# The first samples of a four-layer pipeline get another timetable, and their statistics another place

## The chip, the core and the metric

The kernel runs on one core of a Trainium2 chip. The core's engines work side by side and each has its own list of instructions, which it takes strictly in order: TensorE (PE, matrix products; its weight loads are shown apart as PEld), VectorE (DVE), ScalarE (ACT), GpSimd (POOL), and SyncE (SP), which here only issues DMAs. ACT and POOL issue some DMAs too. The metric is device time in microseconds (us). Three executions of the kernel before took 5671.38, 5691.11 and 5691.64 us, so the median is 5691.11 us.

## The reference

The input x has 16 samples of 64 x 64 positions (4096 tokens) with 256 channels, in float32. Four layers follow one another, each as x = x + layer(group_norm(x)), with 32 groups of channels whose mean and variance run over a whole sample. That is why each layer needs statistics of the whole sample before it can begin.

```
x = x + codebook(gn(x))       # nearest of 1024 codes per token: argmin of the distance, then the code
x = x + rowattention(gn(x))   # f, g, h = x Wf + bf, x Wg + bg, x Wh + bh; sigmoid(f g^T) h along each image row
x = x + gate(gn(x))           # x0, x1, x2 = x w1, x w2, x w3; softmax over n of x0[n] x1[m];
                              # gate = sigmoid(sum_n x2[n] softmax[n, m]); gate * x
x = x + linattention(gn(x))   # q, k, v; softmax of q over a head's channels, of k over tokens;
                              # context = k v^T; context q; W_out; layer norm with gamma and beta
```

## The kernel before

A sample's tokens are worked on in 8 chunks of 512. Each sample goes through seven stages, and each stage is a Python generator that emits some instructions and yields a number of steps:

- **statistics** (`stats0`): loads the 8 chunks of the input, 512 KB each, on SP's queue into the pool `xb` (4 buffers), two `bn_stats` of VectorE per chunk (L266), then `gn_finish` (L270 to L299) on all engines, with small matrix products and a `pow` on GpSimd. Its result, `norm0[b]`, is needed by the search of that sample.
- **search** (`stage1`, L330 on): per tile of 128 tokens four products of 128 x 512 (L403), ScalarE's bias (L398), VectorE's maximum and its index (L409, L414), and an indirect DMA on POOL's queue that adds the chosen code to the token (L415). `back` (L371 on) transposes the sums (L378), takes their statistics and stores them. 32 tiles.
- **layer 1** (`layer1`, L436 on): the row attention, matrix products L482, L493, L513 and L533, and one VectorE addition per chunk (L538). It loads chunk `ch + 2` when chunk `ch` is done, into a pool of 3 buffers (`xm`).
- **rows** (`rows2`): the three rows x0, x1, x2. It loads the 8 chunks again, into the same pool `xb` as the statistics.
- **exps** (`stage2`): 64 times ScalarE's exponential of 128 x 2048 elements (L645) and VectorE's weighted sum (L648).
- **gate** (`gate2`): multiplies x by its gate (L702, L703).
- **layer 3** (`stage3`): the linear attention, most of its work in matrix products (L765, L782, L902, L908).

A planner at the end of the program gives each stage of each sample a start and a length on a clock of its own, whose unit is one search: search b runs from b to b + 1. A stage starts at its ready time or when the same stage of the sample before ends, whichever is later. A heap then always advances the generator that is due first, by its yield times length over total. So the planner decides the order of the program, not times. The order is a priority: the framework builds each engine's list from it by taking, in a model of the machine, the earliest instruction in program order that is ready. The constants: layer 1 begins 0.06 after its search and takes 0.7 (0.2 for sample 0), rows 0.1, the exponentials start 0.17 after layer 1's end and take 1.0, the gate 0.8, layer 3 1.0. `FILL` places the statistics of samples 1 to 7 (two from 0.05 to 0.95, three from 1.0 to 1.27, two from 1.4 to 1.58). Those of samples 8 to 15 start at b - 0.7 and take 0.5.

With these numbers the first exponentials are due from 1.43 to 2.43, those of sample 1 from 2.93 to 3.93 (they wait for layer 1 of that sample), and from then on the exponentials of one sample follow those of the other without a gap.

Of the kernel before, what the change touches and what calls it, by code (L numbers as in the profile page):

```python
# [22 lines left out]
NCHUNK = NT // CH  # L23
CW = CH * P
# [9 lines left out]
LAGR = 0.03  # L34
# [3 lines left out]
LEN3 = {0: 0.4, 1: 0.33, 2: 0.37}  # L38
FILL = ((0.05, 0.95, 2), (1.0, 1.27, 3), (1.4, 1.58, 2))
EARLY = sum(n for _, _, n in FILL)  # L40


@with_exitstack
def kernel(
# [265 lines left out]

    norm0 = {}

    def stats0(b):
        tag = f"s0_{b}"
        st = stats_tile(0, f"st_{tag}")
        src = xT[b].rearrange("(k p) n -> p k n", p=P)
        for ch in range(NCHUNK):
            xt = xb.tile([P, NK, CW], F32, tag="xb", name=f"xs_{tag}_{ch}")
            nc.sync.dma_start(out=xt, in_=src[:, :, ch * CW : (ch + 1) * CW])
            chunk_stats(st, xt, ch)  # L320
            yield 1.5
        with tc.high_priority(offset=URGENT):
            norm0[b] = gn_finish(st, "n0", b)
        yield 2


    x1_d, norm1 = {}, {}

    def stage1(b):
# [6 lines left out]
        def load(ch):  # L336
            xt[ch] = xa.tile([P, NK, CW], F32, tag="xa", name=f"xt_{tag}_{ch}")
            nc.sync.dma_start(out=xt[ch], in_=src[:, :, ch * CW : (ch + 1) * CW])

# [53 lines left out]
        for ch in range(NCHUNK):  # L393
            for t in range(CH):
# [24 lines left out]
                )  # L419
                yield 4  # L420
                if t == 1 and ch > 0:
                    back(ch - 1)
                    yield 2
# [17 lines left out]
    def layer1(b):  # L441
# [9 lines left out]
        def load(ch):  # L451
            xt[ch] = xm.tile([P, NK, CW], F32, tag="xm", name=f"xt_{tag}_{ch}")
            nc.sync.dma_start(out=xt[ch], in_=x1[ch])

# [95 lines left out]
        for ch in range(NCHUNK):  # L550
            if ch > 0:
                store(ch - 1)
            if ch + 1 < NCHUNK:
                yield from attend(ch + 1)
                yield 2
            mix(ch)
            yield 3
        store(NCHUNK - 1)
# [373 lines left out]
    tasks, free = [], {}  # L932
    b = 0
    for begin, end, n in FILL:
# [11 lines left out]
    for b in range(nb):  # L946
# [3 lines left out]
        task("search", b, 1.0, stage1(b), 160)  # L950
        end = task("layer1", b + 1 + LAG1, (LEN1 if b else 0.2) if left else 0.35, layer1(b), 88)
        task("rows", end + LAGR, 0.1, rows2(b), 8)
        if left:
            end = task("exps", end + LAG2, 1.0, stage2(b), 160)
            end = task("gate", end + LAG3, 0.15 if left == 1 else LENG, gate2(b), 36)
        else:
            end = task("exps", end + LAG2, 0.65, stage2(b, NCHUNK), 200)
# [47 lines left out]
```

## Time and profile before

| | |
|---|---|
| median of three executions | 5691.11 us (5671.38 to 5691.64) |
| the profiled execution | 5674.06 us, span 5672.1 us |
| TensorE / VectorE / ScalarE / GpSimd busy | 91% / 89% / 81% / 32% of the span |
| mean granted clock of TensorE | 0.962 |
| moved by DMA | 1059.26 MB, 187 GB/s over the span |
| exponentials of sample 0 begin, end | 322 us, 584 us |
| exponentials of sample 1 begin | 713 us |
| exponentials of sample 15 begin, end | 5224 us, 5507 us |

In the lines of the profile an instruction is named by its line in the kernel (L403), its engine, and its tiles as out<-in. A row of a table by stretches has the beginning and end of the stretch in us from the span's start, its length, the busy time of PE, PEld, DVE, ACT and POOL with the number of instructions in brackets, the granted clock of TensorE as a share of full speed, the mean busy share of the 16 DMA engines, and what they moved in GB/s. Where the table is of one tile alone, only the engines that touch it are listed. Durations of groups are merged busy time.

### The profile page before, as it was taken

How to read it: one execution, taken by the hardware profiler on the slowest of the kernel's cores; microseconds unless marked ns; L12 is line 12 of the kernel's file. 1: busy time of each engine (PE TensorE's matmuls, PEld its weight loads, DVE VectorE, ACT ScalarE, POOL GpSimd, SP SyncE). 2: the span in 40 equal slices, each digit the busy share in tenths (PEclk: the TensorE clock that was granted, in tenths of full speed). 3: DMA queues.
4: the chain of work that ended last, by engine and by line, in shares of the span. 5: the costliest groups of instructions: out<-in, count | busy, mean ns of one | idle time of the engine just before them, and what ended most of it. 6: DMA issues, size and time to landing. Idle time of an engine off the chain costs nothing.

```text
span 5672.1 us, 76096 instructions
## 1 busy us (share of the span) xinstructions
PE 5162.0 (91%) x26927; PEld 3189.6 (56%) x26927; DVE 5049.3 (89%) x7186; ACT 4571.1 (81%) x6642; POOL 1801.5 (32%) x1076
## 2 busy tenths in 40 slices
PE   7977889989999999999999999999999999987788
PEld 3534446545656566565655656565565656564556
DVE  7589799899999999999999999999999999988882
ACT  4468589888989898888978888898888879887873
POOL 2223234323333333334333333333333333321221
PEclk9988999999999999999999999999999999998889
DMA  8553744655665757566575656657575675745543
GB/s 254 174 178 84 232 115 144 214 163 185 196 198 175 224 159 236 171 211 198 185 234 155 216 185 200 210 173 236 160 224 183 201 219 156 222 149 176 200 157 119
DMA packets 521365, 1059.26 MB, mean 187 GB/s; under 512 B 52504, under 2 KB 266392, under 8 KB 512792
## 3 DMA queue, kind: packets, MB, share of 16 engines
q1 hardware_dynamic: 406288, 885.11, 46.5%
q0 software_dynamic: 73728, 67.14, 8.3%
q10 hardware_dynamic: 40968, 102.13, 4.6%
q8 instruction: 214, 3.51, 0.3%
q14 instruction: 167, 1.37, 0.1%
HBM read 751.18 MB, written 303.04 MB: 186 GB/s over the span
## 4 chain that ended last, share of the span: by engine, by line
PE 46%; DVE 17%; ACT 16%; issue 6%; DMA 5%; POOL 4%; SPq 0%; ACTq 0%; DVEq 0%; POOLq 0%
PE pd_s L403 14%; ACT ex_s L645 7%; DVE ex_s L648 7%; PE ph_l L493 4%; PE pxo_s L908 3%; PE pqv_s L782 3%; PE po_l L533 2%; PE pk_s L765 2%; ACT nn_s L398 2%; POOL qv_s L802 2%; PE pz_s L857 2%; DVE i_s L414 2%; DVE nn_s L409 2%; PE pxo_s L902 2%; PE pvr_s L865 2%
## 5 line engine op out<-in xcount | busy, mean ns | idle before, releaser
L648 DVE CUSTOM_DVE_ANT_0 ex_s<-ex_s,x2b 128x2048 f32<-128x2048 f32 x1024 | 2360.4, 2312 | 77.6 <-ACT ex_s L645 74.6
L645 ACT ACTIVATE ex_s<-x0b,nmax_s,x_r 128x2048 f32<-128x2048 f32 x1024 | 2138.6, 2089 | 40.7 <-DVE num_s L648 30.5
L403 PE MATMUL pd_s<-e,xn_s 128*128 128x512 f32 x4096 | 1971.1, 614 | 43.9 <-DVE m L409 27.9
L415 POOL DMA_INDIRECT xc_s<-in_emb_rows,i_s x512 | 1113.7, 2175 | 1852.7 <-DVE i_s L414 1337.5
L403 PEld LDWEIGHTS pd_s<-e,xn_s 128*128 128x128 f32 x4096 | 745.8, 195 | 778.8 <-issue 669.1
L409 DVE CUSTOM_DVE_ANT_0 nn_s<-pd_s,nn_s 128x1024 f32<-128x1024 f32 x512 | 619.9, 1212 | 113.5 <-PE pd_s L403 63.0
L414 DVE FIND_INDEX8 i_s<-m,nn_s 128x8 uint32<-128x1024 f32 x512 | 622.9, 1217 | 0.0
L398 ACT ACTIVATE nn_s<-ne,nx_s 128x1024 f32<-128x1024 f32 x512 | 582.5, 1143 | 33.1 <-DVE nx_s L369 18.7
L493 PE MATMUL ph_l<-wh_l,xt_l 128*128 128x256 f32 x2048 | 519.6, 390 | 28.7 <-DVE m L409 16.9
L782 PE MATMUL pqv_s<-wqv_s,xk_s 128*128 128x256 f32 x2048 | 489.3, 381 | 0.0
L493 PEld LDWEIGHTS ph_l<-wh_l,xt_l 128*128 128x128 f32 x2048 | 379.7, 192 | 138.9 <-issue 69.0
L782 PEld LDWEIGHTS pqv_s<-wqv_s,xk_s 128*128 128x128 f32 x2048 | 389.1, 191 | 120.6 <-issue 59.7
L802 POOL TENSOR_TENSOR qv_s<-qv_s,qm_s 128x512 f32<-128x512 f32 x128 | 221.6, 1731 | 662.6 <-DVE qm_s L801 363.2
L868 POOL TENSOR_TENSOR lrs_s<-lrs_s,mhalf 128x4 f32<-128x4 f32 x128 | 178.0, 1391 | 677.2 <-ACT lrs_s L867 663.3
L756 POOL TENSOR_TENSOR qv_s<-qv_s,qd_s 128x512 f32<-128x512 f32 x128 | 214.4, 1675 | 249.0 <-DVE qd_s L755 132.0
L533 PE MATMUL po_l<-blk,h_l 128*128 128x128 f32 x2048 | 282.1, 288 | 3.0 <-DVE m L409 1.5
L533 PEld LDWEIGHTS po_l<-blk,h_l 128*128 128x128 f32 x2048 | 260.6, 200 | 41.1 <-issue 24.5
L908 PE MATMUL pxo_s<-wctx_s,qo_s 128*128 128x256 f32 x1024 | 269.2, 386 | 2.2 <-DVE qo_s L876 2.2
L765 PE MATMUL pk_s<-xk_s,wk_s 128*128 128x512 f32 x512 | 256.0, 620 | 1.0 <-DMA xk_s<-x_g 0.9
L913 ACT COPY y_s<-pxo_s 128x512 f32<-128x512 f32 x256 | 147.5, 580 | 132.4 <-PE pxo_s L912 116.0
L378 PE MATMUL pt_s<-ident,xc_s 128*128 128x128 f32 x1024 | 156.7, 282 | 105.2 <-DMA xc_s<-in_emb_rows,i_s 79.0
L351 ACT ACTIVATE sq_s<-xt_s,first 128x512 f32<-128x512 f32 x256 | 200.2, 806 | 37.2 <-DMA x0b<-rows_r 21.0
(206 smaller groups left out, 7322.0 us busy)
## 6 DMA issues: line engine op xcount, KB each, us to landing
xs_s<-in_xT SPq DMA_DIRECT2D x128, 512.0 KB
xt_s<-in_xT SPq DMA_DIRECT2D x128, 512.0 KB
xc_s<-in_x SPq DMA_DIRECT2D x128, 512.0 KB
x_s<-xt_s ACTq DMA_DIRECT2D x128, 512.0 KB
xt_l<-x_s SPq DMA_DIRECT2D x128, 512.0 KB
x_l<-xt_l SPq DMA_DIRECT2D x128, 512.0 KB
xr_r<-x_l SPq DMA_DIRECT2D x128, 512.0 KB
xg_g<-x_l SPq DMA_DIRECT2D x128, 512.0 KB
```

What stands on the lines that cost most here:

```text
L398: nc.scalar.activation(nn, ne2, AF.Identity, bias=nx2[ch][:, t : t + 1])
L403: nc.tensor.matmul(pd[:, cols], lhsT=xn[ch][:, k, t * P : (t + 1) * P], rhs=e2[:, k, cols], start=(k == 0), stop=(k == NK - 1),)
L409: nc.vector.tensor_tensor_reduce(out=nn, in0=pd, in1=nn, scale=1.0, scalar=-3.0e38, op0=ALU.add, op1=ALU.max, accum_out=m8[:, 0:1],)
L414: nc.vector.max_index(i8, m8, nn)
L415: nc.gpsimd.indirect_dma_start(out=xc[ch][:, t, :], out_offset=None, in_=emb_rows, in_offset=bass.IndirectOffsetOnAxis(ap=i8[:, 0:1], axis=0),
L493: nc.tensor.matmul(ph[:, t, :], lhsT=X[:, k, t * P : (t + 1) * P], rhs=wh_n[:, k, :], start=(t % 2 == 0 and k == 0), stop=False, skip_grou ...
L533: nc.tensor.matmul(po[:, m : m + P], lhsT=h[:, t, k * P : (k + 1) * P], rhs=at[:, t, :, :].rearrange("p r i -> p (r i)"), start=True, stop ...
L645: nc.scalar.activation(ex, x0b, AF.Exp, bias=nmax[:, T : T + 1], scale=x01[:, T, 1:2], accum_out=den[:, h, T : T + 1])
L648: nc.vector.tensor_tensor_reduce(out=ex, in0=ex, in1=x2b, scale=1.0, scalar=0.0, op0=ALU.mult, op1=ALU.add, accum_out=num[:, h, T : T + 1],)
L765: nc.tensor.matmul(pk, lhsT=wk_n[:, k, :], rhs=xt[:, k, :], start=(k == 0), stop=(k == NK - 1))
L782: nc.tensor.matmul(pqv[:, j, :], lhsT=xt[:, k, t * P : (t + 1) * P], rhs=wqv_n[:, k, :], start=(j == 0 and k == 0), stop=False, skip_group ...
L908: nc.tensor.matmul(px[:, j, :], lhsT=qT[:, t * P : (t + 1) * P], rhs=wctx[:, 1, :], start=False, stop=False, skip_group_check=True,)
```

## The change

A table `RAMP` gives the first four samples their own numbers: the distance of layer 1 from its search, the length of layer 1, the length of rows, the distance of the exponentials from layer 1's end, and the length of the exponentials. On the planner's clock the exponentials of samples 0 to 3 now run from 1.31 to 2.56, 2.56 to 3.76, 3.76 to 4.90 and 4.90 to 5.98, each beginning where the one before ends. Layer 1 of samples 0 to 3 takes 0.15, 0.3, 0.45 and 0.58. From sample 4 on the numbers are the old ones, and exponentials, gate and layer 3 are due 0.05 later than before.

`FILL` is empty. The statistics are advanced from within sample 0's own stages: those of sample 1 from `stage1`, one step after certain tiles (9 steps within the first 28 tiles); those of samples 2 to 5 from `layer1`, 4 or 5 steps after each chunk (36 steps over 8 chunks). The loads of these statistics are tied on SP's queue behind the newest load of the search or of layer 1 (`issue_after`), so that they can't be issued ahead of it. The statistics of samples 6 and 7 now start at b - 0.7 like the later ones.

```diff
-FILL = ((0.05, 0.95, 2), (1.0, 1.27, 3), (1.4, 1.58, 2))
-EARLY = sum(n for _, _, n in FILL)
+RAMP = {0: (0.03, 0.15, 0.05, 0.13, 1.25), 1: (0.04, 0.3, 0.06, 0.14, 1.2), 2: (0.05, 0.45, 0.08, 0.16, 1.14), 3: (0.06, 0.58, 0.1, 0.17, 1.08)}
+FILL = ()
+BESIDE = (1, 4)
+EARLY = sum(BESIDE) + sum(n for _, _, n in FILL)
...
-    norm0 = {}
-
-    def stats0(b):
+    norm0, marks = {}, {}
+
+    def behind(name):
+
+        return tc.issue_after(marks[name]) if name in marks else nullcontext()
+
+    def stats0(b, after=None):
...
-            nc.sync.dma_start(out=xt, in_=src[:, :, ch * CW : (ch + 1) * CW])
+            with behind(after):
+                nc.sync.dma_start(out=xt, in_=src[:, :, ch * CW : (ch + 1) * CW])
...
+    beside = {
+        "search": chain.from_iterable(stats0(b, "search") for b in range(1, 1 + BESIDE[0]) if b < nb),
+        "layer1": chain.from_iterable(stats0(b, "layer1") for b in range(1 + BESIDE[0], 1 + sum(BESIDE)) if b < nb),
+    }
+
+    def advance(name, b, n):
+
+        for _ in range(n if b == 0 else 0):
+            next(beside[name], None)
...
-            nc.sync.dma_start(out=xt[ch], in_=src[:, :, ch * CW : (ch + 1) * CW])
+            marks["search"] = nc.sync.dma_start(out=xt[ch], in_=src[:, :, ch * CW : (ch + 1) * CW]).ins
...
                 yield 4
+                advance("search", b, ((T + 1) * 9 * BESIDE[0]) // 28 - (T * 9 * BESIDE[0]) // 28)
...
-            nc.sync.dma_start(out=xt[ch], in_=x1[ch])
+            marks["layer1"] = nc.sync.dma_start(out=xt[ch], in_=x1[ch]).ins
...
             mix(ch)
+            advance("layer1", b, ((ch + 1) * 9 * BESIDE[1]) // NCHUNK - (ch * 9 * BESIDE[1]) // NCHUNK)
             yield 3
...
-    b = 0
+    b = sum(BESIDE)
...
-        end = task("layer1", b + 1 + LAG1, (LEN1 if b else 0.2) if left else 0.35, layer1(b), 88)
-        task("rows", end + LAGR, 0.1, rows2(b), 8)
+        early, len1, lenr, early2, lenx = RAMP.get(b, (LAG1, LEN1, 0.1, LAG2, 1.0))
+        end = task("layer1", b + 1 + early, len1 if left else 0.35, layer1(b), 88)
+        task("rows", end + LAGR, lenr, rows2(b), 8)
...
-            end = task("exps", end + LAG2, 1.0, stage2(b), 160)
+            end = task("exps", end + early2, lenx, stage2(b), 160)
```

More of the change, by code (lines that the diff above doesn't have):

```diff
@@ L1 @@
 import heapq
-from contextlib import ExitStack
+from contextlib import ExitStack, nullcontext
+from itertools import chain
 import concourse.bass as bass
```

## The prediction

> **What bounds the kernel now.** I read first the page's head and its busy shares: TensorE (PE) is busy for 5162 us and VectorE (DVE) for 5049 us of a span of 5672.1 us, so neither leaves much to the other. Then I cut the span where one stage's work begins or ends. The marks are the first exponential of each sample (ScalarE's timeline: 322, 713, 1013, 1309, 1629, 1953, 2286 us, ... 5224 us for the last), the end of sample 0's exponentials (584 us) and the beginning of the second search (182 us).
>
> ```profile
> span 5672.1 us, 76096 instructions
> PE 5162.0 (91%) x26927; PEld 3189.6 (56%) x26927; DVE 5049.3 (89%) x7186; ACT 4571.1 (81%) x6642; POOL 1801.5 (32%) x1076
> ```
>
> The same stretches, busy time of each engine, granted clock, DMA share, GB/s:
>
> ```profile
> 38.00:182.00 144.00, 129.69 (x476) 60.48 (x475) 124.19 (x217) 69.85 (x93) 52.06 (x36) 0.99 0.83 240
> 182.00:322.00 140.00, 134.43 (x830) 81.11 (x830) 67.78 (x116) 60.33 (x118) 22.92 (x24) 0.96 0.55 178
> 322.00:585.00 263.00, 189.23 (x766) 94.68 (x765) 250.34 (x324) 214.85 (x259) 81.89 (x39) 0.87 0.40 117
> 585.00:713.00 128.00, 116.12 (x565) 61.25 (x564) 86.29 (x147) 64.50 (x102) 28.05 (x21) 0.97 0.79 252
> 713.00:1013.00 300.00, 277.96 (x1412) 162.66 (x1411) 274.02 (x380) 263.30 (x373) 105.17 (x56) 0.95 0.47 140
> 1013.00:1309.00 296.00, 266.43 (x1390) 156.95 (x1389) 280.29 (x372) 257.94 (x350) 89.57 (x48) 0.95 0.61 190
> 1309.00:1629.00 320.00, 309.03 (x1673) 192.66 (x1672) 304.42 (x432) 284.10 (x413) 113.44 (x64) 1.00 0.62 194
> 1629.00:1953.00 324.00, 311.71 (x1672) 193.69 (x1671) 304.04 (x428) 283.83 (x412) 113.93 (x64) 0.99 0.62 191
> 1953.00:2286.00 333.00, 317.30 (x1684) 197.52 (x1683) 315.07 (x446) 284.71 (x415) 112.83 (x66) 0.98 0.64 198
> 5224.00:5507.00 283.00, 217.09 (x995) 153.99 (x994) 240.14 (x351) 225.71 (x341) 71.27 (x46) 0.86 0.50 169
> ```
>
> The reader is to see an engine that changes. The first search is TensorE's. Layer 1 of sample 0 is TensorE's alone (134 of 140 us, VectorE half idle). The first exponentials are VectorE's (250 of 263 us, TensorE at 72% and its clock at 0.87). Then come 128 us without exponentials, in which VectorE idles for 42 us. From 1309 us on both are at 95%. VectorE's work on the tile of the statistics, by stretch:
>
> ```profile
> 38.00:182.00 144.00, 41.15 (x62) 0.99 0.83 240
> 182.00:200.00 18.00, 6.11 (x10) 0.81 0.57 168
> 322.00:585.00 263.00, 20.13 (x32) 0.87 0.40 117
> 1953.00:2286.00 333.00, 10.43 (x16) 0.98 0.64 198
> ```
>
> Sixteen instructions are one sample, about 10 us. Four of the seven early samples lie beside the first search, two in the stretch that VectorE bounds. A stretch with one sample of statistics takes 333 us, the one before it without took 324.
>
> **The work of a sample.** The groups' busy times, added by stage and scaled so that they meet the page's totals (TensorE's groups add up to 5836 us against 5162, factor 0.885; VectorE's 0.928, since groups overlap), over 16 samples. TensorE: search 2282 x 0.885 / 16 = 126 us; layer 1 with its norms and the rows pass 1400, 77 us; layer 3 2154, 119 us. VectorE: search 1510 x 0.928 / 16 = 88; layer 1 and norms 367, 21; exponentials 2485, 144; gate 367, 21; layer 3 565, 33; statistics 167, 10.
>
> **Check against before.** The planner's clock counts searches: search b runs from b to b+1. Before, the exponentials of sample 0 run from 1.43 to 2.43, those of sample 1 from 2.93 to 3.93, then one sample per unit without a gap. For each stretch I take the larger of the two engines' work. To 1: 126 (measured 144). To 1.43: 0.43 x 126 + 77 = 131 (140). To 2.43: VectorE 88 + 144 + 0.53 x 21 + 2 x 10 = 263 (263). To 2.93, the pause: 0.5 x 126 + 0.47 x 77 = 99 (128). To 3.93: VectorE 282 (300). To 4.93: 290 (296). Then 322 (320) and 322 (324). The sum is 1835 against 1915 measured between 38 and 1953 us. The 80 us on top are 18 in the first search, 9 in layer 1, 29 in the pause, 18 and 6 in the two stretches behind it.
>
> **The change, part by part,** up to the start of sample 5's exponentials. That is 6.98 on the new clock, 6.93 before; seven samples have their statistics by then in both.
>
> Statistics beside the first search: one sample instead of four. That takes 3 x 10 us of VectorE and 24 loads of 512 KB from a stretch whose DMA share is 0.83. TensorE waited 11.5 us there for gathered rows. The work left is TensorE's, so at most its 14 us of idle time go: between 0 and 14, I take 6, since the gather's wait is the part that traffic can lengthen. 138 us.
>
> Layer 1 of sample 0 (1.00 to 1.31 instead of 1.43): TensorE 0.31 x 126 + 77 = 116, plus the 9 seen before, 125. Four samples of statistics come in: 64 VectorE instructions, 40 us, under a VectorE that was busy for 68 of 140 us and loses 0.12 x 88 = 11. They are covered. Their 32 loads are less sure. The stretch moved 178 GB/s x 140 us = 24.9 MB; 0.12 of a search less is about 2 MB (1059 MB / 16 = 66 MB a sample, a quarter of it the search's); 32 loads of 512 KB less what of the old ones lay there add some 14. That is 37 MB; at 268 GB/s, the rate of the 50 us with the highest DMA share that held statistics loads, 138 us; at 313, the best slice, 118. I take 133, between the two bounds; ends 123 and 150.
>
> The Trainium skill, "DMA: Bandwidth & Descriptors", section Specifications, gives about 358 GB/s as a core's share of HBM. By that figure 37 MB would take an estimated 103 us, TensorE would decide, and this sum would be 8 us lower; no slice of this trace reaches it.
>
> Exponentials of sample 0 (1.31 to 2.56): VectorE 1.25 x 88 + 144 + 21 = 275, no statistics any more. TensorE 1.25 x 126 + 77 = 234. Layer 1 of sample 1 is now pressed into 2.04 to 2.34, and taken alone that part is TensorE's (0.34 x 126 + 70 = 113 against 89 on VectorE). In three parts the sum is 140 + 113 + 44 = 297. I take 290, near the upper end, since the pause showed that such alternation is not smoothed; ends 278 and 306.
>
> Exponentials of samples 1 to 4: 2.56 to 3.76, VectorE 1.2 x 88 + 21 + 144 + 21 + 10 = 302, plus 12 (18 and 6 before), 314. To 4.90: TensorE 1.14 x 126 + 77 + 0.94 x 119 = 333, plus 4, 337. To 5.98: TensorE 325, VectorE 322 with one statistics, plus 11 (333 measured for 322 and 317), 336. To 6.98: 314 plus 11, 325.
>
> A load of the statistics is issued on SP's queue behind the newest load of the search or of layer 1, and is itself held until VectorE frees one of four buffers; whatever SP issues next (the search's loads and tokens, layer 1's stores, the rows pass, which uses the same buffers) stands behind it. In the first search these issues waited 60.0 us for VectorE in 23 waits, 2.6 us each, and TensorE did not feel it. I price it at nothing: layer 1 loads two chunks ahead. If that cover is gone, it is the slower rival below.
>
> The Trainium skill, "SBUF — State Buffer", section "SBUF: two separate sides", says of DMAs issued from GpSimd that their descriptors starve while VectorE holds a port shared with it. In this trace TensorE waited 45.4 us for gathered rows between 330 and 585 us, where VectorE was at 95%, and 11.5 us in the first search; the rule speaks against longer exponentials beside the search. By it 45 x 1.25 = 56 us would be waited for by TensorE, which is what it has spare (290 - 234), so the sum would stay.
>
> **Sum.** 138 + 133 + 290 + 314 + 337 + 336 + 325 = 1873, against 1915: 42 us earlier, to a point where 0.05 of a search and layer 1 more is done. Behind it the clocks run alike (11.09 units to the end), with exponentials, gate and layer 3 0.05 later against the search. At the end no search covers that: 0.05 x 283 us, the last exponentials' stretch, is 14. Of that I take 12: from nothing, if VectorE's 43 us idle there absorb it, to 17 us, 0.05 of the last 697 us per 2.02 units. The profiled execution took 5674.06 us, 2 more than its span: 5674 - 30 = 5644. It lay 17 us under the median of three, 5691.11, and 3 over the fastest; I put the forecast between the two readings (5644 and 5661): 5652.
>
> **Rivals.** (1) No change within 0.5%: layer 1 at its DMA bound (150), the first exponentials at 306, and the planner's pause replaced by a new alternation, as the 297 warns: 30 - 17 - 16 is a loss of 3, 5677 to 5694, say 5682. For it speaks that VectorE's idle time before the first exponentials stays much the same: both the search's share and 20 us of statistics leave it. Against it, TensorE and VectorE are both better covered after 2.56. (2) Slower: SP's queue in layer 1 of sample 0. Between 26 and 199 us 40 loads of statistics were issued, 4.3 us apart. If the 32 new ones keep that pace and the 24 others of layer 1 and rows, 2 us each, add to it instead of filling in, the stretch takes 138 + 48 = 186 us and more, and every wait of VectorE for a chunk holds the search behind it; at 200 the gain of 30 is a loss of 37, 5674 + 37 = 5711 to 5728, say 5720. It decides from a stretch of about 190 us on. Against it: DVE waited for such a load for only 12.0 us in the whole run. (3) The change does not do what it says: instructions run ahead wherever an engine is free, so sample 0's exponentials end early as before and the pause comes back as idle VectorE time; then only the earlier start stays, 6 + 7 us, 5661 to 5678, say 5668.
>
> **How the numbers follow.** What a measurement of this kernel can tell is about 0.5%, 28 us. Chances: forecast 0.47, rival 1 0.20, rival 2 0.20, rival 3 0.13. Rival 3 and a shift of the steady stretches by 0.05, which no row prices (2 us per stretch over ten would be 20), fall on both sides of that line. So faster by over 0.5% 0.49, within it 0.28, slower 0.23. The range: with all lower ends (130, 123, 278, and 5 less in each of the other four) the sum is 50 us less, 5594 on the profiled execution and 5611 on the median, so 5600; upwards it takes in rival 1 and reaches to rival 2's 5720. The forecast's own range is 5610 to 5665.
>
> **What the profile after would show.** The statistics' tile: 16 instructions up to about 176 us, 64 in the next 133 us, none until about 1250. DMA share there near 0.9 instead of 0.55. First exponentials of the samples near 309, 599, 913, 1250, 1586 and 1911 us. No stretch of 100 us without an exponential before 5100. VectorE's idle time from 585 to 713 gone, and TensorE's clock above 0.87 during sample 0's exponentials. I am wrong if the first exponential comes after 340 us, if long waits of the DMA queue on the statistics appear in layer 1, or if the stretches after 1911 are longer than 335.

## The result, and the profile after

The changed kernel takes 5739.32 us (median of six executions, 5719.06 to 5744.57), the kernel before 5682.09 us (six executions, 5665.41 to 5691.64). The ratio is 1.0098, with a 95% interval from 1.0075 to 1.0122: slower by 1%. The prediction was 5652 us, its range 5600 to 5720.

The profiled execution of the changed kernel took 5719.06 us, the fastest of the six; the one of before took 5674.06. So the traces explain 45 of the 57 us between the medians, and everything that follows is told in those 45. The head of the page after:

```profile
span 5717.2 us, 76163 instructions
PE 5175.7 (91%) x26927; PEld 3211.8 (56%) x26927; DVE 5063.6 (89%) x7186; ACT 4575.3 (80%) x6642; POOL 1745.5 (31%) x1076
```

The work is the same: TensorE is busy for 13.7 us more, VectorE for 14.3 us, in a span that is 45 us longer. The time went into idle stretches of both. I cut the span at the first exponential of each sample, as for the kernel before. They now come at 333, 641, 956, 1301, 1651, 1986, 2328 us, ... 5026 and 5284 us; before, at 322, 713, 1013, 1309, 1629, 1953, 2286, ... 4958 and 5224. The table by stretches, columns as in the prediction:

```profile
38.00:181.00 143.00, 127.40 (x458) 59.27 (x457) 101.70 (x175) 68.96 (x90) 50.82 (x34) 0.97 0.57 154
181.00:333.00 152.00, 132.37 (x796) 80.95 (x794) 83.38 (x144) 54.26 (x110) 19.35 (x23) 0.92 0.67 224
333.00:590.00 257.00, 201.31 (x912) 105.62 (x913) 234.12 (x292) 222.26 (x270) 73.61 (x34) 0.89 0.38 107
590.00:641.00 51.00, 51.00 (x255) 26.37 (x254) 34.12 (x61) 22.87 (x42) 12.64 (x11) 1.00 0.70 232
641.00:956.00 315.00, 270.49 (x1286) 146.52 (x1285) 293.69 (x399) 269.69 (x361) 98.80 (x50) 0.92 0.55 169
956.00:1301.00 345.00, 329.97 (x1727) 203.09 (x1726) 318.85 (x451) 293.05 (x425) 121.56 (x70) 0.98 0.60 186
1301.00:1651.00 350.00, 328.16 (x1738) 203.72 (x1737) 323.51 (x465) 290.30 (x421) 121.68 (x69) 0.99 0.63 195
1651.00:1986.00 335.00, 312.87 (x1651) 193.03 (x1650) 314.26 (x447) 284.32 (x410) 107.44 (x65) 0.98 0.63 198
1986.00:2328.00 342.00, 319.28 (x1682) 199.83 (x1681) 312.45 (x445) 284.84 (x413) 102.56 (x67) 0.97 0.62 193
5284.00:5557.00 273.00, 211.17 (x958) 150.59 (x957) 245.57 (x347) 222.39 (x334) 68.06 (x44) 0.85 0.50 167
```

Three things are to be seen. The pause between the exponentials of samples 0 and 1 (590 to 641) shrank from 128 to 51 us. The exponentials of sample 0 (333 to 590) did not get longer: 257 us, before 263. And the four stretches behind them (641 to 1986) take 1345 us where they took 1240, with TensorE busy for 92% and VectorE for 93% of them, before 94% each. Before, TensorE had used the pause to work ahead (116 of 128 us busy) and the next stretches were short, 300 and 296 us. TensorE's work in the pause and the four stretches together is 1281 us before and 1292 after. The pause was time of TensorE's that the change moved rather than won.

The rows of the statistics' tile (VectorE alone) show that the placement was done as the diff says: 22 instructions in the first search, 56 beside layer 1, none beside sample 0's exponentials, and 16 each for samples 6 and 7 later.

```profile
38.00:181.00 143.00, 14.63 (x22) 0.97 0.57 154
181.00:333.00 152.00, 34.89 (x56) 0.92 0.67 224
333.00:590.00 257.00, 0.00 (x0) 0.89 0.38 107
...
1301.00:1651.00 350.00, 10.51 (x16) 0.99 0.63 195
1651.00:1986.00 335.00, 10.39 (x16) 0.98 0.63 198
```

The 45 us divide into three:

| part | before | after | difference |
|---|---|---|---|
| start to sample 5's first exponential | 1953 us | 1986 us | +33 |
| nine steady samples, 5 to 14 (one sample) | 3005 us (333.9) | 3040 us (337.8) | +35 |
| from sample 14's first exponential to the end | 714 us | 691 us | -23 |

In the nine steady samples both kernels do the same with the same instructions; only the planner's times of exponentials, gate and layer 3 are 0.05 of a search later. The whole stretch in one row, of the kernel before:

```profile
1953.00:4958.00 3005.00, 2836.25 (x15133) 1768.06 (x15132) 2815.36 (x3990) 2559.80 (x3723) 1029.14 (x592) 0.98 0.63 197
```

and of the changed kernel:

```profile
1986.00:5026.00 3040.00, 2844.12 (x15116) 1780.60 (x15115) 2821.16 (x3987) 2559.15 (x3717) 994.00 (x593) 0.97 0.62 194
```

TensorE is idle for 3005.00 - 2836.25 = 169 us before and for 196 us after: 27 of the 35 us are idle time, 8 are matrix products that took longer. What TensorE waited for in this stretch (who waited <- for what; us in total, times, the longest; pg_n at L285 before and L288 after is the group norm's first product), before:

```profile
PE px_s L357 <- ACT sq_s L351: 22.0, 26, 2.2
PE prt_r L602 <- ACT rows_r L597: 15.4, 8, 2.6
PE pxt_s L364 <- ACT xrow_s L362: 15.3, 25, 1.6
```

and after:

```profile
PE pg_n L288 <- DVE mv_n L284: 45.1, 9, 5.0
PE pd_s L421 <- DVE gate_s L676: 32.2, 8, 5.6
PE pc_s L827 <- ACT ek_s L815: 27.9, 28, 2.3
PE prt_r L622 <- ACT rows_r L617: 24.0, 9, 2.7
```

The two waits at the head of the list come once in nearly every sample, and neither was among the long ones before. The first is the group norm behind a search, which needs the statistics of that search's last chunk. One of its nine places in the timeline (start, duration; in brackets the idle time before it and the instruction that ended it):

```profile
2679.09 1.04 PE L396 MATMUL pt_s<-ident,xc_s 128*128 128x128 f32 x8
...
2680.86 1.06 ACT L399 COPY xt_s<-pt_s 128x512 f32<-128x512 f32 x2
2681.08 2.23 DVE L668 CUSTOM_DVE_ANT_0 ex_s<-ex_s,x2b 128x2048 f32<-128x2048 f32 x1
2683.23 1.28 DVE L269 BATCH_NORM_STATS2 st_s<-xt_s 128x6 f32<-128x512 f32 x2
2684.43 0.59 DVE L284 BATCH_NORM_AGGREGATE mv_n<-st_s 128x2 f32<-128x48 f32 x2
2685.16 0.56 PE L288 MATMUL pg_n<-mv_n,dmat 128*128 128x2 f32 x2 [5.04 <-DVE mv_n L284]
```

TensorE ends the last transposes at 2680.1 us and has the norm's product next in its list. ScalarE copies the transposed chunk until 2681.9 us, and VectorE has one of the 64 exponential sums in front of the chunk's statistics, until 2683.3 us. Statistics and norm's input take the rest. So TensorE stands for 5 us: some 1.8 for the copy, 1.4 for the sum, 1.9 for the statistics. In the kernel before, TensorE's list has products of the next search (L403) between the two. At the same place, sample 8:

```profile
2648.66 1.04 PE L378 MATMUL pt_s<-ident,xc_s 128*128 128x128 f32 x8
2649.53 3.60 PE L403 MATMUL pd_s<-e,xn_s 128*128 128x512 f32 x8
2652.96 0.28 PE L285 MATMUL pg_n<-mv_n,dmat 128*128 128x2 f32 x2
```

(A product of the search leaves two records in the profile, so these eight are four products.) The norm's product then waits for nothing.

### The profile page after: what moved, and what is told of

Same layout as the page of the kernel before. It is cut to its first block, busy times and chain, and to the rows that moved or that the text cites. A ratio compares the mean times of both kernels' runs of the same rounds, so it can differ in the third digit from the quotient of the medians.

```text
span 5717.2 us, 76163 instructions
## 1 busy us (share of the span) xinstructions
PE 5175.7 (91%) x26927; PEld 3211.8 (56%) x26927; DVE 5063.6 (89%) x7186; ACT 4575.3 (80%) x6642; POOL 1745.5 (31%) x1076
## 5 line engine op out<-in xcount | busy, mean ns | idle before, releaser
L433 POOL DMA_INDIRECT xc_s<-in_emb_rows,i_s x512 | 1066.4, 2083 | 2049.2 <-DVE i_s L432 1191.7
L512 PE MATMUL ph_l<-wh_l,xt_l 128*128 128x256 f32 x2048 | 510.6, 390 | 4.6 <-DVE m L427 2.8
L802 PE MATMUL pqv_s<-wqv_s,xk_s 128*128 128x256 f32 x2048 | 504.0, 387 | 1.9 <-ACT xt_s L399 1.9
L512 PEld LDWEIGHTS ph_l<-wh_l,xt_l 128*128 128x128 f32 x2048 | 380.7, 192 | 109.5 <-issue 40.0
L888 POOL TENSOR_TENSOR lrs_s<-lrs_s,mhalf 128x4 f32<-128x4 f32 x128 | 201.6, 1575 | 535.2 <-ACT lrs_s L887 535.1
L785 PE MATMUL pk_s<-xk_s,wk_s 128*128 128x512 f32 x512 | 281.6, 671 | 0.0
L776 POOL TENSOR_TENSOR qv_s<-qv_s,qd_s 128x512 f32<-128x512 f32 x128 | 180.7, 1412 | 322.7 <-DVE qd_s L775 228.3
L552 PE MATMUL po_l<-blk,h_l 128*128 128x128 f32 x2048 | 265.1, 280 | 5.7 <-DVE m L427 2.5
L366 ACT ACTIVATE xn_s<-xt_s,first 128x512 f32<-128x512 f32 x256 | 202.2, 806 | 55.0 <-PE pd_s L421 32.9
```

Source lines behind the costliest of these rows:

```text
L433: nc.gpsimd.indirect_dma_start(out=xc[ch][:, t, :], out_offset=None, in_=emb_rows, in_offset=bass.IndirectOffsetOnAxis(ap=i8[:, 0:1], axis=0),
L512: nc.tensor.matmul(ph[:, t, :], lhsT=X[:, k, t * P : (t + 1) * P], rhs=wh_n[:, k, :], start=(t % 2 == 0 and k == 0), stop=False, skip_grou ...
L552: nc.tensor.matmul(po[:, m : m + P], lhsT=h[:, t, k * P : (k + 1) * P], rhs=at[:, t, :, :].rearrange("p r i -> p (r i)"), start=True, stop ...
L785: nc.tensor.matmul(pk, lhsT=wk_n[:, k, :], rhs=xt[:, k, :], start=(k == 0), stop=(k == NK - 1))
L802: nc.tensor.matmul(pqv[:, j, :], lhsT=xt[:, k, t * P : (t + 1) * P], rhs=wqv_n[:, k, :], start=(j == 0 and k == 0), stop=False, skip_group ...
```

## The experiments

In each comparison "steady" is the mean distance between the first exponentials of one sample and the next, from sample 5 to sample 14: 333.9 us before, 337.8 us after. Times are medians; the ratio is to the kernel before on the same chip, with its 95% interval.

### Is it the 0.05? The changed kernel with exponentials of sample 3 shorter by 0.05

```diff
-RAMP = {..., 3: (0.06, 0.58, 0.1, 0.17, 1.08)}
+RAMP = {..., 3: (0.06, 0.58, 0.1, 0.17, 1.03)}
```

From sample 4 on all due times are then those of before, and everything else of the change stays.

> The changed kernel with one number altered: the exponentials of sample 3 take 1.03 instead of 1.08 on the planner's clock, so that from sample 4 on all stages stand to each other as in the kernel before. Theory A (the exponentials, gate and layer 3 that come 0.05 later are what makes a steady sample last 338 us instead of 334): the distance from one sample's first exponential to the next goes back to about 334 us from sample 5 on, 9 x 4 = 35 us less in all, about 5705 us. Theory B (the loss arises before sample 5's exponentials, from the statistics' new place, and the steady distance only follows from it): the distance stays near 338 and the time near 5739 us.

5696.21 us, 1.0026 [1.0013, 1.0040]; steady 334.0. The whole steady stretch, first exponential of sample 5 to that of sample 14:

```profile
1982.00:4987.00 3005.00, 2836.02 (x15133) 1764.92 (x15132) 2817.46 (x3987) 2556.80 (x3723) 1022.98 (x592) 0.99 0.63 197
```

That is the row of before: 3005 us, TensorE busy for 2836 and idle for 169. Of the 57 us between the medians 43 are gone. The traces show less, 24 of 45 us, since this kernel's end takes 706 us, 8 less than before and 15 more than in the changed kernel. Up to sample 5 the kernel is as late as the changed one, 1982 us.

### The 0.05 alone, in the kernel before

```diff
-LAG2 = 0.17
+LAG2 = 0.22
```

> The kernel before with one number altered: the exponentials of every sample start 0.22 instead of 0.17 after layer 1, so that exponentials, gate and layer 3 come 0.05 later against the search, and nothing else moves. Theory A (that place makes the steady sample longer): the distance between first exponentials is about 338 us from sample 5 on, and the time 5682 + 35 = about 5717 us. Theory B (the loss comes from the first samples): the distance stays near 334, the time within 15 us of 5682.

5737.31 us, 1.0104 [1.0088, 1.0121]; steady 338.0, with the changed kernel's waits of TensorE (1998 to 5040 us):

```profile
PE pg_n L285 <- DVE mv_n L281: 45.1, 9, 5.0
PE pd_s L403 <- DVE gate_s L656: 34.3, 8, 5.4
```

One number, none of the change's new code, and the kernel before loses 55 us. Not all of it is the steady samples': in the traces 45 us lie before sample 5's first exponential (1998 us instead of 1953), where the first samples got the later due times too, 37 in the nine steady samples, and the end is 18 shorter (696 us). In the traces that keep the old place behind sample 5 the end takes 706 to 716 us, so the larger part of the changed kernel's gain at the end belongs to the 0.05. From both sides, then: the shift of 0.05 makes the loss in the steady samples, 334.0 us each without it and 338.0 with it alone.

### The parts of the change apart

The timetable without the new place of the statistics:

```diff
-FILL = ()
-BESIDE = (1, 4)
+FILL = ((0.05, 0.95, 2), (1.0, 1.27, 3), (1.4, 1.58, 2))
+BESIDE = (0, 0)
```

> Only the new timetable: statistics of samples 1 to 7 where they were before. Theory A (steady place) expects the steady distance at 338 us, and a first part that is shorter than that of the changed kernel by the two samples of statistics that now lie beside sample 3's and 4's search, 2 x 10 us: about 5719 us. Theory B (statistics beside layer 1) expects the first exponential near 310 us instead of 333, no loss, and about 5680 us or less.

5727.25 us, 1.0079 [1.0062, 1.0096]; steady 338.6; first exponentials at 338, 650, 974, 1320, 1670 and 2001 us.

The same with sample 3's exponentials 1.03 long, as above:

> The new timetable for the first four samples, with sample 3's exponentials at 1.03 so that the steady place is the old one, and the statistics of seven samples where they were before. If the three parts add up (place of the steady stages 43 to 55 us, statistics about 12), the timetable alone is worth between -10 and +5 us: 5672 to 5688. The prediction's sum for it was a gain of some 30 us, so about 5650 us. If the new timetable itself costs, it stays above 5700 us.

5691.84 us, 1.0011 [0.9999, 1.0024]; steady 334.0; first exponentials at 340, 652, 974, 1320, 1655 and 1988 us.

The statistics without the timetable (sample 0 with the numbers of before, and none for samples 1 to 3):

```diff
-RAMP = {0: (0.03, 0.15, 0.05, 0.13, 1.25), 1: ..., 2: ..., 3: ...}
+RAMP = {0: (0.06, 0.2, 0.1, 0.17, 1.0)}
```

> Only the new place of the statistics: the timetable of before for all samples. Theory A (steady place) expects the steady distance at 334 us, and a loss of the two samples of statistics that come later (20 us) and of the later first exponential (10 us): about 5705 us. Theory B (all the loss is the statistics') expects the whole loss, about 5739 us, and the first exponential at 333 us or later.

5694.83 us, 1.0017 [1.0003, 1.0031]; steady 334.6; first exponentials at 342, 707, 1009, 1306, 1637 and 1972 us.

So apart from the 0.05 no part brings anything: the timetable alone +10 us with an interval that reaches no change, the statistics alone +12, both together +14. In all of them the first exponential comes at 338 to 342 us instead of 322. The timetable takes the stretch to sample 1 from 391 to 312 us, and then needs 322, 346, 335 and 333 us where 300, 296, 320 and 324 stood: 79 us won, 96 lost, and 18 lost at the start.

### Do samples 6 and 7 cost the stretches of samples 3 and 4?

The first of the kernels above (exponentials 1.03 long) with two samples of statistics put back beside sample 0's exponentials, so that seven are early again:

```diff
-FILL = ()
+FILL = ((1.4, 1.58, 2),)
```

> The changed kernel with the steady place of before (1.03) and the statistics of samples 6 and 7 back in the stretch of the first exponentials (1.4 to 1.58 on the planner's clock); samples 1 to 5 stay beside the first search and layer 1. If the 12 us of the statistics are those two samples' VectorE time in the stretches of samples 3 and 4, the time falls by 10 to 20 us against the same kernel without this, to 5676 to 5686 us. If they are the blocked rows pass beside layer 1 (its loads came at 300 us instead of 220), nothing changes: about 5696 us, with the first exponential still near 335 us.

5714.67 us, 1.0060 [1.0044, 1.0077]; steady 334.1, first exponentials at 342, 669, 992, 1336, 1670 and 1999 us. It is 18 us slower, where the expectation had a gain or nothing: the two samples cost more early, between 342 and 669 us, than beside samples 3 and 4.

### Which of the shifted stages is it?

In the kernel before, the exponentials later and layer 3 where it was:

```diff
-LAG2 = 0.17
-LAG3, LENG = 0.06, 0.8
+LAG2 = 0.22
+LAG3, LENG = 0.06, 0.75
```

> The kernel before with exponentials and the gate's beginning 0.05 later, but the gate 0.75 long instead of 0.8, so that layer 3 keeps its place against the search. With everything 0.05 later the steady sample lasts 338 us, against 334 in the kernel before. If the exponentials' place does it (VectorE's list has them in front of what the next search needs), the distance stays near 338 us and the time near 5735. If layer 3's place does it (TensorE has no layer-3 products to do while it waits for the norm after the search), the distance is 334 us and the time about 5700 or less.

5749.47 us, 1.0128 [1.0114, 1.0143]; steady 338.4. And layer 3 alone later:

```diff
-LAG4 = 0.04
+LAG4 = 0.09
```

> The kernel before with layer 3 alone 0.05 later (0.09 instead of 0.04 after the gate); exponentials and gate stay. If layer 3's place makes the steady sample longer, the distance is near 338 us and the time near 5720 or more. If the exponentials' place does it, the distance stays at 334 us and the time within 15 us of 5682.

5716.28 us, 1.0064 [1.0046, 1.0082]; steady 337.3. Either alone makes the steady sample longer by about as much as both together.

### Is there a slope? Other distances in the kernel before

One constant each: `LAG2` 0.135, 0.155, 0.185 and 0.27 instead of 0.17, and layer 3 earlier, `LAG4` 0.02 instead of 0.04.

> The kernel before with exponentials 0.135 after layer 1 instead of 0.17, so exponentials, gate and layer 3 stand 0.035 earlier against the search. If the steady sample gets longer the later they come, it gets shorter here: 331 to 333 us, and the time 5655 to 5675. If what counts is that certain ends do not meet, and 0.17 happens to lie well, it is 334 us or longer, 5682 us or more.

> The kernel before with exponentials 0.155 after layer 1 (0.17 before; steady distances: 340 us at 0.135, 334 at 0.17, 338 at 0.22, 352 at 0.27). If the distance changes smoothly with the place, it is near 336 to 337 us here and the time near 5705. If every small shift gives another order of the lists with a cost of its own, the distance can be anything from 332 to 341.

> The same at 0.185. Smooth: a distance near 335 us, the time within 15 us of 5690. Another order with a cost of its own: anything from 332 to 341, and neighbours that do not lie on a line.

> The kernel before with the exponentials 0.27 after layer 1 instead of 0.17; exponentials, gate and layer 3 stand 0.10 later against the search, so that a sample's exponentials begin after the end of a search and no more just before it. Steady distances so far: 340 us at 0.135, 334 at 0.17, 338 at 0.22. If what costs is that the two ends meet, the distance is back at 334 or less here. If later is worse, it is 340 us or more and the time 5750 or more.

> The kernel before with layer 3 alone 0.02 earlier (0.02 instead of 0.04 after the gate). Layer 3 alone 0.05 later took 337 us per steady sample. Smooth with an optimum at 0.04 or below: 333 to 335 us, 5670 to 5690. Another order with a cost of its own: not to be told, within 332 to 341.

| exponentials behind layer 1 | layer 3 behind the gate | steady, us | time, us | ratio |
|---|---|---|---|---|
| 0.135 | 0.04 | 340.2 | 5755.00 | 1.0131 [1.0113, 1.0149] |
| 0.155 | 0.04 | 343.7 | 5809.39 | 1.0225 [1.0203, 1.0246] |
| 0.17 (before) | 0.04 | 333.9 | - | 1 |
| 0.185 | 0.04 | 334.0 | 5718.84 | 1.0065 [1.0045, 1.0085] |
| 0.22 | 0.04 | 338.0 | 5737.31 | 1.0104 [1.0088, 1.0121] |
| 0.27 | 0.04 | 352.4 | 5861.77 | 1.0326 [1.0311, 1.0341] |
| 0.17 | 0.02 | 349.5 | 5862.24 | 1.0311 [1.0290, 1.0331] |
| 0.17 | 0.09 | 337.3 | 5716.28 | 1.0064 [1.0046, 1.0082] |

There is no slope. A shift of 0.015 down costs 10 us per sample, the same shift up nothing, and layer 3 earlier by 0.02 costs more than four times what 0.05 later does. Two of the distances, 343.7 and 349.5, lie outside what their expectations allowed (332 to 341). With 0.185 the loss is elsewhere: sample 5's exponentials begin at 1996 us instead of 1953. That is so in all seven: they reach sample 5 at 1988 to 2011 us, so 35 to 58 us of each trace lie before the steady samples, and the times do not follow from the distances alone. No kernel on record reaches sample 5 earlier than the one before; its numbers lie well at both places. Other waits lead each list. With 0.155 (2008 to 5101 us):

```profile
PE pd_s L403 <- DVE m L409: 61.6, 19, 6.5
```

With layer 3 earlier (2011 to 5156 us):

```profile
PE pq_s L744 <- POOL qv_s L756: 51.6, 9, 5.8
PE pwt_s L845 <- DVE wctx_s L840: 42.9, 9, 5.3
```

They recur once or twice per sample again, each time at another place.

### Is it the wait for the norm?

Three kernels, each made from the one with the exponentials 0.05 later (steady 338.0). In the first the last transposes and statistics get the norm's urgent priority:

```diff
-        back(NCHUNK - 1)
         with tc.high_priority(offset=URGENT):
+            back(NCHUNK - 1)
             norm1[b] = gn_finish(st1, "n1", b)
```

> The kernel before with the exponentials 0.05 later (it took 5737 us), and the last chunk of each search (its transposes, copies and statistics) given the same urgent priority as the norm behind it. In the later place TensorE stood for 5.0 us per sample at the norm's first product, waiting for VectorE's statistics of that chunk, which an exponential's sum had been put in front of. If that wait is what makes the steady sample 338 us long, it goes, the steady distance falls to 334 and the time to about 5700 us. If the wait only shows a delay that VectorE or ScalarE would have anyway, the wait goes and the distance stays at 338 us, 5730 to 5740 us.

5752.33 us, 1.0130 [1.0111, 1.0149]; steady 337.8. The wait at L285 is still 45.1 us in 9 times, so this tells nothing of what it costs. In the other two the norm comes later in the program and without priority, so that products of layer 3 and of the next search stand between, five steps later here and eight in the second:

```diff
-        with tc.high_priority(offset=URGENT):
-            norm1[b] = gn_finish(st1, "n1", b)
+        yield 5
+        norm1[b] = gn_finish(st1, "n1", b)
```

> The kernel before with its exponentials 0.05 later (5737 us, steady distance of first exponentials 338.0 us, with a TensorE wait of 5.0 us once per sample for the last chunk's statistics, L285), and here the norm behind the search is emitted five steps later and without its urgent priority, so that about nine matrix products of layer 3 and of the next search stand in TensorE's list between the last transposes and the norm's product. If that recurring wait carries the 4 us per sample: the wait at L285 falls below 1.5 us, the steady distance returns to 333.5 to 335 us and the total to about 5690 to 5705. If the wait is only where a general lag of the engines shows: the wait at L285 goes, another one takes its place, and the steady distance stays at 337 to 340 us, the total at 5730 to 5755.

> The same with eight steps instead of five: four products of the next search and some of layer 3 stand between. If the wait at L285 carries the cost: steady distance 333.5 to 335 us as with five steps, both alike. If any new order is a new draw: the two differ from one another by 2 us per sample or more, or both stay at 337 us and more though the wait is gone. Layer 1 then begins its norm some 8 us later, which may cost up to 10 us once at the first sample.

With five steps: 5715.91 us, 1.0076 [1.0054, 1.0098]; steady 336.3. The wait at L285 is gone, and these lead the list from 1998 to 5025 us:

```profile
PE pd_s L403 <- DVE gate_s L656: 31.3, 8, 4.8
PE ph_l L493 <- DVE wh_l L308: 23.3, 9, 2.6
```

The second of them is layer 1's weights, scaled by the norm that comes later now. With eight steps: 5697.62 us, 1.0048 [1.0032, 1.0065]; steady 334.9, though most of the wait is still there (1990 to 5004 us):

```profile
PE pg_n L285 <- DVE mv_n L281: 32.9, 9, 3.7
PE pd_s L403 <- DVE gate_s L656: 30.9, 8, 4.8
```

Neither alternative of the first expectation came true, and the two kernels are not alike as the second had it, nor 2 us apart: without the wait 1.7 us per sample are won, not 4, and with three quarters of it 3.1. So 5 us of this wait are not 5 us of a sample, and the wait for the gate, which both have as the changed kernel has it, does not keep a kernel from 334.9 either. Where the norm stands matters; which stall carries the 4 us is not settled. TensorE's idle time in the steady stretch was 197 us with the exponentials later, 177 with five steps and 185 with eight, its busy time 2845, 2850 and 2829: a part of the differences lies in products that take longer, and no run isolates why.

### Why do the first exponentials begin late?

In the changed kernel the rows' loads of sample 0 were issued from 300 us on, behind 32 loads of statistics that share four buffers with them. From the kernel with the exponentials 1.03 long, first the rows' loads of sample 0 in another pool:

```diff
-                xt = xb.tile([P, NK, CW], F32, tag="xb", name=f"xr_{tag}_{h}_{j}")
+                pool, ptag = (xg, "xg") if b == 0 else (xb, "xb")
+                xt = pool.tile([P, NK, CW], F32, tag=ptag, name=f"xr_{tag}_{h}_{j}")
```

> The changed kernel with the steady place of before (1.03 for sample 3's exponentials; 5696 us, first exponential at 340 us), and the rows pass of sample 0 loads into the gate's two buffers, which nothing else uses then, instead of those of the statistics. Its eight loads came at about 300 us and later, behind the 32 of the statistics, instead of from 220 us on. If the wait for those buffers delays the first exponentials, they begin at 310 to 322 us and the time falls by up to 15 us, to 5680 to 5690 us. If the first exponentials wait for something else (DMA as a whole, or GpSimd's reduction before them), they stay after 330 us and the time at about 5696.

5714.68 us, 1.0069 [1.0055, 1.0083]; the first exponential at 352 us, the rows' loads from 221 to 336 us. Then the statistics beside layer 1 in that pool, in the same manner:

> The changed kernel with the steady place of before (5696 us, first exponential at 340 us), and the statistics beside layer 1 loaded into the gate's two buffers; the rows pass has its four to itself. Putting the rows pass into those two buffers brought its loads from 304 to 221 us, but the last came at 336 and the first exponential at 352. If the shared buffers delay the first exponentials, they begin at 325 us or earlier here, and the time is 5680 to 5690. If DMA as a whole delays them, they stay at 335 to 345 and the time near 5696. If only two buffers slow the statistics, the first exponential is as now, and search 2 or 3 comes later.

5704.62 us, 1.0044 [1.0028, 1.0060]; the first exponential at 348 us, the rows' loads from 215 to 332 us. In both the first loads come more than 80 us earlier than from the shared buffers and the exponentials later, so the shared buffers are not the cause. The traces show where the delay is. Layer 1 ends with VectorE's aggregation of its statistics (st_l, L284), from which the norm for the rows is made. In the changed kernel seven statistics instructions of an early sample stand in front of it, though layer 1's own are done at 299.1 us:

```profile
299.02 4.23 DVE L269 BATCH_NORM_STATS2 st_s<-xs_s 128x6 f32<-128x512 f32 x7
303.44 0.31 DVE L284 BATCH_NORM_AGGREGATE mv_n<-st_l 128x2 f32<-128x48 f32 x1
```

Before, layer 1's statistics are done at 291.1 us and the aggregation follows at once. So it comes 12 us later: 8 us are layer 1 itself, 4 these statistics. From there to the first exponential the changed kernel takes no longer than the one before:

| kernel | aggregation | first exponential | between |
|---|---|---|---|
| before | 291.1 us | 322.3 us | 31 us |
| changed | 303.4 us | 332.6 us | 29 us |
| changed, 1.03 | 310.0 us | 339.6 us | 30 us |
| rows in the other pool | 307.8 us | 352.1 us | 44 us |
| statistics in the other pool | 318.6 us | 348.2 us | 30 us |
| timetable alone | 286.0 us | 338.4 us | 52 us |

With the statistics in two buffers, VectorE waits for their loads, and the aggregation stands behind them until 318.6 us. With the rows in two buffers, it is TensorE that waits for the rows' loads behind the aggregation, 2.0 and 5.3 us. No run moves the aggregation alone; these shares are read from the traces.

With the timetable alone no statistics delay the aggregation. What comes late there lies behind it: GpSimd is late with the maximum over the rows that the exponentials need (L649). Its timeline there:

```profile
319.68 1.60 POOL L433 DMA_INDIRECT xc_s<-in_emb_rows,i_s  x1 [0.70 <-DVE ext_s L647]
321.59 1.56 POOL L433 DMA_INDIRECT xc_s<-in_emb_rows,i_s  x1 [0.30 <-issue]
329.59 0.37 POOL L649 PARTITION_ALL_REDUCE ab_s<-ext_s  x1 [6.44 <-issue]
```

VectorE takes the rows' extremes from 319.3 us on. GpSimd then issues two gathers of the search that stand ahead in its list, and after the second it needs another 6.44 us before the reduction; the first exponential is at 338.4 us. Before, the same 7 us lay between a gather and the reduction, but they had mostly passed when the extremes came at 314.3 us, and the first exponential followed 8 us after them. This gap is in every sample: all 16 reductions of the kernel before start 5.9 to 7.7 us after GpSimd's instruction before them. Had the reduction followed the extremes as it did before, by 2.4 us, it would have come 8 us earlier; by this reckoning about half of the 16 us in this kernel is the order on GpSimd's list. No run changed that order, and the rest stays open.

## Why the prediction was wrong

The forecast for the profiled execution was 5644 us, and it took 5719. Three parts make the 75 us: the sum to sample 5 was 75 us too low, the nine steady samples took 35 us more than forecast, and the end took 35 us less (23 shorter instead of 12 longer). That the last two cancel is luck.

**The sum to sample 5 was 75 us too low.** The seven terms against the measurement, in us:

| stretch | predicted | measured |
|---|---|---|
| first search | 138 | 143 |
| layer 1 of sample 0 | 133 | 152 |
| to sample 1's exponentials | 290 | 308 (257 and a pause of 51) |
| to sample 2's | 314 | 315 |
| to sample 3's | 337 | 345 |
| to sample 4's | 336 | 350 |
| to sample 5's | 325 | 335 |
| sum | 1873 | 1948 |

The larger engine's work was 333, 325 and 314 us in the last three stretches by the prediction, and 330, 328 and 314 as measured. So there the work was right, and what failed is the allowance for idle time: 4, 11 and 11 us became 15, 22 and 21. In layer 1 and beside the first exponentials TensorE's work was forecast too low as well (116 us, measured 132; 234, measured 252). From 38 us to sample 5's first exponential TensorE was idle for 180 us before and for 194 after, VectorE for 224 and 244. The forecast took away idle time where the pause had been and did not let it return where the stretches got fuller. The timetable alone shows it: 79 us won in the pause, 96 lost behind it. Idle time returned in the first search (VectorE idle for 20 us before, 41 after, since the statistics that had filled it were gone) and behind sample 0.

**"Exponentials of sample 0 (1.31 to 2.56)" was the wrong picture.** They did not stretch over 1.25 searches. This is the third rival's mechanism: ScalarE and VectorE ran ahead, 257 us long, and a pause of 51 us stayed. Its price, an earlier start by 6 and 7 us, did not come, since the first exponential came 11 us later instead. The waits for gathered rows that the prediction feared there did not grow: 37.9 us from 333 to 641 us, where it had 56 by estimate and the kernel before 45.4.

**Layer 1 was mis-sized, 133 us against 152, and the loads were not why.** The second rival, a pile-up on SP's queue, did not happen. SP's waits from 181 to 333 us, of which the second line is the statistics' loads:

```profile
SPq L564 <- DVE xt_l L557: 48.1, 7, 22.9
...
SPq L327 <- DVE st_s L269: 8.1, 10, 2.0
```

The stretch moved 224 GB/s x 152 us = 34 MB, near the 37 estimated, at a DMA share of 0.67. It stayed below the rate used for this term, 268 GB/s, and its last 15 us ran at 320, so that rate did not set its length. The step that failed is "They are covered". It counted the statistics' VectorE instructions and their loads, and left out two things: the norm that ends each sample of them, which has products in TensorE's list, and the order on VectorE's list, which put 4 us of them in front of the end of layer 1 (above). TensorE's waits from 181 to 333 us:

```profile
PE pg_n L288 <- DVE mv_n L284: 10.2, 5, 3.0
```

Before, from 182 to 322 us:

```profile
PE pg_n L285 <- DVE mv_n L281: 1.2, 1, 1.2
```

Nine us more of the same kind of wait that appears in the steady samples: 7.2 us at the norms of samples 2 to 5, and 1.8 more at the norm of the search itself (3.0 instead of 1.2). The norms of three early samples lay in this stretch before, too, and TensorE did not wait at them. The rest is TensorE's work: the stretch held 80 of the 256 records of a search's products, 0.31 as planned, and took 38 us for them, but beside them 94 us of other work where the forecast had the mean of 77 (before, 86 beside 49). Some products were slower: those of L501 took 445 ns each instead of 410 (L482 before). The granted clock was 0.92 instead of 0.96, but those of L512 took 385 ns instead of 395 (L493 before), so the clock alone does not explain it.

**A figure that the trace of before comes up to.** The prediction also said that no slice of the trace of before reaches the 358 GB/s that the Trainium skill, "DMA: Bandwidth & Descriptors", section Specifications, gives for a core. The prediction had looked at slices of 50 us. From 302 to 322 us the trace has 367 GB/s:

```profile
302.00:322.00 20.00, 20.00 (x75) 7.83 (x74) 7.69 (x17) 7.74 (x12) 3.25 (x4) 1.00 1.03 367
```

The share of 1.03, above the whole, shows that transfers at the edges count too much in so short a slice; begun 2 us earlier, it has 342 GB/s at a share of 1.00. So this trace reaches rates of about that size for 20 us, and tells no more.

**The first search was right in its mechanism and wrong in its 6 us.** TensorE waited there for gathered rows for 12.4 us (11.5 before). With 24 loads fewer in the stretch the wait for the gather was not shorter.

**"Behind it the clocks run alike" is the second step that failed.** It priced the shift of exponentials, gate and layer 3 by 0.05 at nothing, and it cost 35 us in nine samples. The text had named it as a thing that no row prices and guessed at 20 us on either side. The experiments show the shift as the cause from both sides (334.0 us per steady sample without it, 338.0 with it alone); which stall or slower product carries the 4 us stays open. Without it the change would have been within 0.5% of before, and not a gain: the ramp's error above is shown by that kernel too, which reaches sample 5 at 1982 us.

**The tail had the wrong sign.** "0.05 x 283 us ... 12" was added for exponentials that no search covers. Measured are -23 us, and -18 with the shift alone. A likely reason, which no run isolates: the exponentials still to be done from there are the same, while 0.05 of a search less is left to do beside them.

**Signs.** Of the three that were to show the forecast wrong, the third came: the stretches after 1986 us are longer than 335. The first exponential (333 us, forecast 309) and SP's queue stayed inside their limits. The statistics' tile (22 and 56 instructions, forecast 16 and 64) is near the forecast, and TensorE's clock beside sample 0's exponentials (0.89, above 0.87) is as forecast; the DMA share in layer 1 is not, 0.67 instead of 0.9.

## What to carry to other kernels

Where two engines are at 94% and their lists are built from one order of the program, other due times for a stage are another set of lists for every sample that has them: with moved due times in the steady part the distance from sample to sample went up to 352.4 us here, 18 us more on each of nine samples, while the start to be improved held 128 us of pause once. Six kernels with another start and the old due times behind it kept 333.2 to 334.6 us. So keep the steady part's due times where they are when the start is edited, and read the distance between the same instruction of consecutive samples first: it tells a shift in the steady part from one at the start in one view. And before a pause is counted as a gain, look whether the bounding engine works ahead in it, since then only its idle time is to be won (12 of 128 us here).

## What was not expected of the hardware

The 16 DMA engines moved 342 to 367 GB/s in slices of 20 us (before, the 1 MB broadcasts of the rows, L615, among their transfers) and 320 GB/s for 15 us (after), well over the 268 GB/s that had looked like a bound. On GpSimd 5.9 to 7.7 us lay between the instruction before and each of the 16 reductions over the partitions (before). And the wait of TensorE on one norm, 5 us in every sample, was worth less than its length: with it gone a sample was 1.7 us shorter, and with 3.7 us of it left, in another order, 3.1 us shorter.
